# One order of an attention turn in place of two, with two places for other TensorE work that may stay empty

## The chip, the cores and the metric

The kernel runs on one core of a Trainium2 chip, in one launch. The metric is the time of the launch in microseconds as the device measures it; smaller is better. A core has a matrix engine (TensorE, "PE" in the profile, its weight loads "PEld"), a vector engine (VectorE, "DVE"), an engine for functions of one element (ScalarE, "ACT"), a general one (GpSimd, "POOL") and one that only issues transfers (SyncE, "SP"). Each runs its own instructions in the order in which they stand in its queue; semaphores hold an instruction back until another engine's result is there. TensorE writes its results into PSUM, which has eight banks of 128 x 512 fp32; a bank can be written anew once the engine that reads it is done.

## The reference

Two sequences of 1024 tokens, 512 wide, fp32. A block of the "macaron" kind: half a feed-forward step, attention, half a feed-forward step, each on the layer-normed input and added to the stream.

```python
x = x + 0.5 * ffn(layernorm(x))
x = x + attn(layernorm(x))
x = x + 0.5 * ffn(layernorm(x))

def ffn(x):      # W_base 512x512, 8 experts of rank 16, the best 2 of a softmax router
    probs = softmax(x @ W_router.T); topk_p, topk_i = top_k(probs, 2)
    w = one_hot(topk_i) weighted with topk_p / sum(topk_p)
    h = einsum('td,erd->ter', x, lora_A)
    return x @ W_base.T + b_base + 2.0 * einsum('ter,eor,te->to', h, lora_B, w)

def bitnet_linear(x, weight, scale):
    s = max(mean(abs(weight), axis=1), 1e-8)
    return nan_to_num((x @ sign(weight / s).T) * (s * scale), posinf=1e6, neginf=-1e6)

def attn(x):     # 32 heads of 16, 8 key/value heads, each shared by 4 query heads
    q, k, v = three bitnet_linear of x, split into heads
    p = softmax(q @ k.T / 4)
    return bitnet_linear(p @ v, o_weight, o_scale)
```

The attention matrix has 2 x 32 x 1024 x 1024 entries; everything else is small beside it.

## The kernel before

**Tiles.** A token tile is 128 tokens. Four of them are a group, so there are two sequences `b` with two groups `g` each. Attention is cut into 32 units: one unit is one sequence, one block of 512 queries and one key/value head with its 4 query heads.

**What a unit does.** Scores are made twice. First with the queries in the rows, to find the largest score of each query: 32 `m` tiles of 128 x 512 (`m_tile`, L785), each a single matmul on 64 rows of the array, each read by one VectorE reduce (`m_max`, L793). The maxima of a unit are gathered (`m_gather`), turned by a transpose on TensorE (`m_place`, tile `mp`, L805), copied by VectorE (`mT`) and moved by two DMAs on SP's queue into the rows of `mq` (L811). Then the scores are made again with the keys in the rows: 32 `e` tiles of 128 x 512 (`e_tile`), each of two matmuls into one bank: `e0`, keys against queries (L820), and `e1`, which takes the maxima off (L824). ScalarE reads each with an exponential into SBUF (`es`, L827). At last `A`: the exponentials times the values with a column of ones (`a_part`, L857), 16 matmuls of 32 columns for each pair of parts A0 A1 or A2 A3, into one bank of its own (`av`); when a unit is through, ScalarE copies that bank out (`unit_end`, L835), and only then may the next unit's first `A` write it. Heads with odd and even numbers lie on the upper and lower 64 rows of the array, so that two neighbouring `m` or `e` matmuls can run at the same time.

**Turns.** The loop of `attention` (L890) goes through turns. In turn n there are 8 `m` tiles of step n, 8 `e` tiles (16 matmuls) of step n-5 and four `A` parts of step n-6; four steps make a unit, so a unit's `m`, `e` and `A` overlap with those of its neighbours. Turns 0 to 4 have `m` tiles only (the lead-in), turns 128 to 133 have no `m` tiles any more. A unit's first `e` comes in a turn with n mod 4 = 1, its first `A` in one with n mod 4 = 2, `mp` in one with n mod 4 = 0.

**Banks.** Seven banks are shared by `m`, `e`, `mp` and all other TensorE work (`bank`, L53); the eighth is that of `av`. A new tile gets the bank that was given back longest ago in the program's order. Other work may hold up to two banks during attention (`flow.stock["fb"]`).

**Other work.** Layer norms, feed-forward steps, the projections and their cleaning of non-finite values run as strands, generators that yield the kind of engine they want next and a due time: `P` for TensorE, `v` VectorE, `a` ScalarE, `g` GpSimd, `d` a DMA on SP's queue. `Flow` keeps a counted time `flow.t` in ticks. When the loop calls `flow.offer(kind)`, the first strand that wants this kind, and is due, records its next instructions there. So the order of all queues is fixed when the program is built; nothing is chosen on the chip.

**The order of a turn.** A string gives it: `m0(i)`, `e0(i)`, `e1(i)` are single matmuls, `A0` to `A3` the four parts, `S` is `m_place`, and the letters F (TensorE), V and W (VectorE), C and D (ScalarE) are places where other work is offered; W and D are used only when more than one strand waits. There are two such strings. FULL has F at its front and its end. BARE has none, and begins with A0. At the start of a turn `wants` looks whether a TensorE piece will be due by the time of FULL's last place; if so the turn takes FULL and counts for 64 ticks (`TICK`), else BARE and 50 (`BRIEF`). `places` spreads the ticks over the order by `LOAD`.

**Waits written into the loop.** Before the first `A` of a unit, `until` offers all kinds, tick by tick, until the copy of the last unit's `av` has been recorded. Before a unit's queries and keys are fetched (`place`), `need` does the same until the projections that it reads have been recorded.

After the last turn the remaining strands are played out (`flow.play`), among them the output projection and second feed-forward step of the last group, which need the last unit.

Of the kernel before, what the change touches and what calls it, by code (L numbers as in the profile page):

```python
# [15 lines left out]
P = 128  # L16
D = 512
# [15 lines left out]
def macaron_kernel(ctx: ExitStack, tc: tile.TileContext, x_in, wbT, b_base, wrT, aT, bT,  # L33
                   wqT, q_sc, wkT, k_sc, wvT, v_sc, woT, o_sc, out):
    nc = tc.nc
    B, S, _ = x_in.shape
# [40 lines left out]
    for name, src, n_out in (("k", wkT, P), ("q", wqT, D), ("v", wvT, P), ("o", woT, D)):  # L77
# [5 lines left out]
        else:  # L83
            t = p2.tile([P, KC, GT], F32, tag="k", name=f"w_{name}", bufs=3)
# [36 lines left out]

    TICK, BRIEF = 64, 50
    LATER = {False: dict(Pv=10, Pa=10, PP=0, vP=36, aP=36, gP=40, va=20, av=16, vg=16, ag=14, gv=30,
                         ga=30, gg=0, vv=0, aa=0, dv=50, dg=50, da=50, dd=0, gd=32, vd=26, ad=26,
                         xd=50, dP=60),
# [12 lines left out]
    class Flow:  # L140
# [63 lines left out]
        def offer(self, kind):  # L204
# [12 lines left out]
                    self.settle()  # L217
                    return True
            return False

        def wants(self, kind, by):
            self.settle()
            return any(s.kind == kind and s.at <= by and (kind != "P" or self.lock in (None, s))
                       for s in self.strands)

        def crowd(self, kind):
            return sum(s.kind == kind and s.at <= self.t for s in self.strands)
# [11 lines left out]
    flow = Flow()  # L239
# [413 lines left out]
    def o_proj(b, g, hs, rank, mv, given, fast=False):  # L653
# [39 lines left out]
        for t in range(TG):  # L693
# [7 lines left out]

    FULL = ("V F W m0(3) e0(4) e0(7) e0(2) m0(7) e1(4) e1(7) e1(2) A0 A1 S C e0(6) e0(3) e1(6) "
            "e0(1) m0(4) V e1(1) m0(0) e1(3) A2 A3 m0(1) e0(0) C e0(5) m0(6) e1(5) e1(0) m0(5) D "
            "m0(2) F")
    BARE = ("A0 A1 e0(2) C m0(7) e1(2) e0(3) e0(4) e0(1) m0(0) e1(3) e1(1) C e1(4) m0(1) m0(6) S A2 "
            "A3 m0(3) e0(0) V e0(5) D e1(0) e0(7) e0(6) e1(5) m0(2) e1(7) V e1(6) W m0(5) m0(4)")
    LEAD_IN = ("m0(0) m0(6) m0(1) V m0(7) F C S V m0(4) m0(2) V F C m0(5) V F C V m0(3) V F C V")
    FULL, BARE, LEAD_IN = (  # L710
        [(o[0], int(o[1]) if len(o) > 1 else 0, int(o[3]) if len(o) > 2 else 0)
         for o in t.split()] for t in (FULL, BARE, LEAD_IN))
    LOAD = dict(e=1, m=1, A=4, F=10)

    def places(order, span):
        w = [LOAD.get(o[0], 0) for o in order]
        return [span * sum(w[:i]) // sum(w) for i in range(len(w))]

    at_F = places(FULL, TICK)[FULL.index(("F", 0, 0))]
    TU = NT // 2  # L720
    LEAD = TU + 1
    units = [(b, qb, g) for b in range(B) for qb in range(NQB) for g in range(G)]
# [40 lines left out]
    def place_v(u):  # L763

        b, _, g = units[u]
        v = p2.tile([P, NT, 32], F32, tag="vaug", name=f"vaug{u}", bufs=3)
        flow.pool = max(flow.pool, flow.t) + 5
        nc.gpsimd.memset(v[:, :, HD:32], 1.0)
        nc.gpsimd.tensor_copy(v[:, :, 0:HD], vd[b][:, :, g * HD:(g + 1) * HD])
        st[u]["v"] = v  # L770
# [9 lines left out]
    def m_tile(u, i, end=True):  # L780

        s = st[u]
        h, (qt, kh) = i % REP, m_where(u, i)
        s["m", i] = bank(f"m{u}_{i}")
        nc.tensor.matmul(s["m", i], s["q"][rows_of(h), h // 2, qt * P:(qt + 1) * P],  # L785
                         s["k"][rows_of(h), kh * 512:(kh + 1) * 512], start=True, stop=True)
        if end:
            m_max(u, i)
# [7 lines left out]
    def m_gather(u):  # L796
        mm = sm.tile([P, 4 * REP], F32, tag="mm", name=f"mm{u}", bufs=2)
        nc.vector.tensor_reduce(mm.rearrange("p (h t) -> p h t", h=REP), st[u]["mn"], AX.X, ALU.min)
        st[u]["mm"] = mm
# [14 lines left out]
    def e_tile(u, i, p):  # L814

        s = st[u]
        kt, h = i // REP, i % REP
        if p == 0:
            t = s["e", i] = bank(f"e{u}_{i}")
            nc.tensor.matmul(t, s["k"][rows_of(h), kt * P:(kt + 1) * P], s["q"][rows_of(h), h // 2, :],  # L820
                             start=True, stop=False)
        else:
            t = s["e", i]
            nc.tensor.matmul(t, two_r[rows_of(h), h // 2, :], s["mq"][rows_of(h), :], start=False,  # L824
                             stop=True)
            e = p2.tile([P, 512], F32, tag="es", name=f"es{u}_{i}", bufs=14)
            nc.scalar.activation(e, s.pop(("e", i)), AF.Exp, scale=HD ** -0.5)  # L827
            s["es"][i] = e
# [22 lines left out]
    def a_part(u, kt, half):  # L851
        s = st[u]
        if kt == 0 and half == 0:
            s["av"] = ps_a.tile([P, 512], F32, tag="av", name=f"av{u}")
        cols = slice(half * 256, half * 256 + 256)
        for h in range(REP):
            nc.tensor.matmul(s["av"][32 * h:32 * h + 32, cols], s["v"][:, kt, :],  # L857
                             s["es"][kt * REP + h][:, cols],
                             start=(kt + half == 0), stop=(kt + half == NT))
        if kt == NT - 1 and half == 1:  # L860
            flow.spawn(unit_end(u), -1)

    def todo(n, lead):

        k = n - lead
        return (k // TU, k % TU) if 0 <= k < TU * len(units) else None

    def attention(chains, n0):

        begin, span = flow.t, 0  # L870
        flow.free, flow.lock = False, None
        flow.busy = dict.fromkeys("Pvagd", flow.t)
        flow.stock["fb"] -= 4
        live = []

        def need(*keys):
            until(lambda: set(keys) <= ended)

        def until(cond):
            for _ in range(4000):  # L880
                flow.settle()
                if cond():
                    return
                flow.t += 1
                for kind in "Pvagd":
                    flow.busy[kind] = 0
                    flow.offer(kind)
            raise RuntimeError([(s.rank, s.kind, s.arg) for s in flow.strands])

        for n in range(n0, TU * len(units) + LEAD + 1):  # L890
            begin = flow.t = max(flow.t, begin + span)
            m, e, a = todo(n, 0), todo(n, LEAD), todo(n, LEAD + 1)
            live = [c for c in live if not c.done]
            while chains and len(live) < 3 and chains[0][0] <= n:
                live.append(flow.spawn(chains.pop(0)[1](), 9))
            if e and e[1] == 0:
                need(*[(units[e[0]][0], h, KC + 1) for h in range(NG)])
                place_v(e[0])
            order = (LEAD_IN if not e and not a else FULL if flow.wants("P", begin + at_F)
                     else BARE)  # L900
            span = BRIEF if order is BARE else TICK
            at = places(order, span)

            hold = n % TU == 0 and n // TU
            for pos, (kind, p, i) in enumerate(order):
                flow.t = max(flow.t, begin + at[pos])
                if kind == "m":
                    if m:
                        m_tile(m[0], m[1] * 2 * REP + i)
                elif kind == "e":  # L910
                    if e:
                        e_tile(e[0], e[1] * 2 * REP + i, p)
                elif kind == "A":
                    if a:
                        if a[0] and a[1] == p == 0:
                            until(lambda: "av" not in st[a[0] - 1])
                        a_part(a[0], a[1] * 2 + p // 2, p % 2)
                elif kind == "S":
                    if 0 < hold <= len(units):
                        m_place(hold - 1)  # L920
                    hold = 0
                elif kind == "F":
                    flow.offer("P")
                elif kind in "VW":
                    if kind == "V" or not m or flow.crowd("v") > 1:
                        flow.offer("v")
                elif kind in "CD":
                    if kind == "C" or not e or flow.crowd("a") > 1:
                        flow.offer("a")
                flow.offer("g")  # L930
                if not hold:
                    flow.offer("d")
            if m and m[1] == TU - 1:
                m_gather(m[0])
            if m and m[0] + 1 < len(units) and m[1] == 2:
                b, qb, g = units[m[0] + 1]
                need((b, qb, g // 2), *[(b, h, KC) for h in range(NG)])
                place(m[0] + 1)
        flow.free = flow.after = True
        flow.t = begin + span  # L940
        flow.stock["fb"] += 4
        flow.busy = dict.fromkeys("Pvagd", flow.t)
# [127 lines left out]
```

## Time and profile before

| | |
|---|---|
| median of 3 runs | 1160.85 us (1159.07 to 1164.19) |
| the profiled execution | 1162.21 us, of which 1160.2 us from the first to the last instruction (span) |
| mean granted TensorE clock | 0.968 |
| before turn 5 | 151.2 us |
| turns 5 to 127 | 151.2 to 1061.1 us |
| turns 128 to 133, without `m` | 1061.1 to 1092.5 us |
| after the last `av` matmul | 1092.5 to 1160.2 us |

A turn is taken from its first `m`, `e` or `av` matmul to that of the next turn. Which of the profile's matmuls belongs to which turn follows from the order of the program's TensorE instructions.

In the profile a line gives engine, source line, operation, the tile written and the tiles read, the shape and the count. In a timeline the first two columns are start and duration in us (several like instructions in a row are merged, their count at the end), and a bracket tells how long the engine stood idle before the instruction and what ended that wait. An fp32 matmul is shown as two instructions. The durations of matmuls overlap: 0.39 us is one matmul from its start to its end, while the next ones run in the array already, so distances between starts are the better measure.

### The profile page before, as it was taken

How to read it: one execution, taken by the hardware profiler on the slowest of the kernel's cores; microseconds unless marked ns; L12 is line 12 of the kernel's file. 1: busy time of each engine (PE TensorE's matmuls, PEld its weight loads, DVE VectorE, ACT ScalarE, POOL GpSimd, SP SyncE). 2: the span in 40 equal slices, each digit the busy share in tenths (PEclk: the TensorE clock that was granted, in tenths of full speed). 3: DMA queues.
4: the chain of work that ended last, by engine and by line, in shares of the span. 5: the costliest groups of instructions: out<-in, count | busy, mean ns of one | idle time of the engine just before them, and what ended most of it. 6: DMA issues, size and time to landing. Idle time of an engine off the chain costs nothing.

```text
span 1160.2 us, 21527 instructions
## 1 busy us (share of the span) xinstructions
PE 1068.2 (92%) x8453; PEld 589.0 (51%) x8453; DVE 878.5 (76%) x1694; ACT 669.8 (58%) x1309; POOL 287.6 (25%) x337
## 2 busy tenths in 40 slices
PE   3989679999999999999989899999999999999988
PEld 2446435554455554455555455644445555444544
DVE  5577978787788787778788898698779878874372
ACT  2222238765667566667746568665667766666611
POOL 4142632000110031112163322032011213421161
PEclk9989759999999999999989999999999999999989
DMA  8012453121111123214334342112222411221101
GB/s 272 3 61 77 140 174 105 47 47 47 47 47 47 47 83 118 48 40 106 106 87 144 83 114 57 47 47 56 56 65 64 120 45 36 67 84 47 55 24 50
DMA packets 48686, 87.43 MB, mean 75 GB/s; under 512 B 8760, under 2 KB 11832, under 8 KB 48584
## 3 DMA queue, kind: packets, MB, share of 16 engines
q1 hardware_dynamic: 47176, 83.36, 24.9%
q10 hardware_dynamic: 1152, 2.10, 0.5%
q8 instruction: 66, 1.08, 0.4%
q0 software_dynamic: 256, 0.59, 0.3%
q14 instruction: 36, 0.29, 0.1%
HBM read 51.19 MB, written 34.32 MB: 74 GB/s over the span
## 4 chain that ended last, share of the span: by engine, by line
PE 71%; DVE 18%; DMA 3%; ACT 3%; POOL 2%; issue 2%; SPq 0%; POOLq 0%; DVEq 0%; ACTq 0%
PE av L857 19%; PE m L785 15%; DVE mn L793 9%; PE e L820 9%; PE e L824 7%; PE pbf L444 5%; PE pbs L444 4%; PE po L668 2%; ACT es L827 2%; DMA x<-in_x 2%; PE pq L538 2%; PE pv L555 1%; PE pbf L448 1%; PE pbs L448 1%; PE phs L368 1%
## 5 line engine op out<-in xcount | busy, mean ns | idle before, releaser
L793 DVE TENSOR_REDUCE mn<-m 128x1 f32<-128x512 f32 x1024 | 647.6, 681 | 161.5 <-PE e L824 86.0
L827 ACT ACTIVATE es<-e 128x512 f32<-128x512 f32 x1024 | 542.4, 602 | 305.9 <-PE e L824 254.0
L785 PE MATMUL m<-k 64*128 64x512 f32 x1024 | 365.1, 443 | 27.6 <-DMA k<-kd 12.9
L857 PE MATMUL av<-es,vaug 128*32 128x256 f32 x4096 | 277.7, 389 | 18.9 <-ACT es L827 9.3
L820 PE MATMUL e<-k 64*128 64x512 f32 x1024 | 277.8, 443 | 2.7 <-DVE mn L793 2.5
L785 PEld LDWEIGHTS m<-k 64*128 64x128 f32 x1024 | 169.4, 188 | 175.9 <-DVE mn L793 77.8
L824 PE MATMUL e<-mq,two_r 64*128 64x512 f32 x1024 | 255.7, 399 | 1.9 <-DMA mq<-mT 1.9
L857 PEld LDWEIGHTS av<-es,vaug 128*32 128x32 f32 x4096 | 108.6, 110 | 148.8 <-issue 83.9
L820 PEld LDWEIGHTS e<-k 64*128 64x128 f32 x1024 | 121.8, 187 | 61.2 <-DVE mn L793 33.0
L824 PEld LDWEIGHTS e<-mq,two_r 64*128 64x128 f32 x1024 | 144.3, 187 | 14.4 <-issue 2.4
L444 PE MATMUL pbf<-wb,xTf 128*128 128x512 f32 x128 | 64.7, 636 | 0.0
L444 PE MATMUL pbs<-wb,xTs 128*128 128x512 f32 x128 | 61.4, 607 | 0.0
L459 POOL TENSOR_TENSOR x<-x,hbf 128x512 f32<-128x512 f32 x8 | 10.2, 1280 | 161.8 <-ACT hbf L456 161.8
L439 POOL TENSOR_TENSOR x<-x,bh 128x512 f32<-128x512 f32 x32 | 41.4, 1318 | 3.3 <-ACT xns L311 3.1
L444 PEld LDWEIGHTS pbf<-wb,xTf 128*128 128x128 f32 x128 | 24.4, 202 | 28.9 <-issue 27.8
L444 PEld LDWEIGHTS pbs<-wb,xTs 128*128 128x128 f32 x128 | 23.1, 192 | 27.4 <-issue 25.8
L270 POOL TENSOR_TENSOR ro<-ro,loo 128x512 f32<-128x512 f32 x16 | 20.7, 1294 | 58.2 <-DVE ro L268 51.5
L571 POOL TENSOR_TENSOR z<-z,y 128x512 fp32r<-128x512 f32 x17 | 22.7, 1337 | 49.9 <-ACT y L568 49.8
L568 ACT CAST y<-z 128x512 fp32r<-128x512 f32 x20 | 12.5, 626 | 36.5 <-DVE z L274 34.0
L265 POOL TENSOR_SCALAR loa<-y 128x512 f32<-128x512 f32 x17 | 11.7, 687 | 85.0 <-ACT y L543 84.2
L459 POOL TENSOR_TENSOR x<-x,hbs 128x512 f32<-128x512 f32 x8 | 10.3, 1285 | 88.5 <-ACT hbs L456 88.5
L620 POOL TENSOR_TENSOR an<-an,rb 128x512 f32<-128x512 f32 x15 | 19.7, 1316 | 49.8 <-DMA rb<-rd 49.7
(204 smaller groups left out, 1014.6 us busy)
## 6 DMA issues: line engine op xcount, KB each, us to landing
k<-qd SPq DMA_DIRECT2D x32, 512.0 KB
k<-kd SPq DMA_DIRECT2D x62, 256.0 KB
qd<-y SPq DMA_DIRECT2D x32, 256.0 KB
qd<-z SPq DMA_DIRECT2D x32, 256.0 KB
ad<-avs SPq DMA_DIRECT2D x32, 256.0 KB
x<-in_x SPq DMA_DIRECT2D x16, 256.0 KB
an<-ad SPq DMA_DIRECT2D x15, 256.0 KB
rb<-rd SPq DMA_DIRECT2D x15, 256.0 KB
```

The source lines that it names most:

```text
L439: nc.gpsimd.tensor_tensor(xt[:, t, :], xt[:, t, :], bh, ALU.add)
L444: nc.tensor.matmul(pb, xT[:, c, t * P:(t + 1) * P], wb[:, c, :], start=(c == 0), stop=False)
L448: nc.tensor.matmul(pb, hT[0][:, t * P:(t + 1) * P], lb, start=False, stop=True)
L538: nc.tensor.matmul(pq, w_[:, k, :], xs[j][:, k, :], start=(k + j == 0), stop=(k + j == KC))
L571: (nc.vector if fast else nc.gpsimd).tensor_tensor(lo, o, y, ALU.subtract)
L668: nc.tensor.matmul(po, hs[j][:, c, t * P:(t + 1) * P], wo[:, c, :], start=(c + j == 0), stop=(c + j == KC))
L785: nc.tensor.matmul(s["m", i], s["q"][rows_of(h), h // 2, qt * P:(qt + 1) * P], s["k"][rows_of(h), kh * 512:(kh + 1) * 512], start=True, st ...
L793: nc.vector.tensor_reduce(s["mn"][:, 2 * (h % 2) + h // 2, qt, kh:kh + 1], s.pop(("m", i)), AX.X, ALU.max, negate=True)
L820: nc.tensor.matmul(t, s["k"][rows_of(h), kt * P:(kt + 1) * P], s["q"][rows_of(h), h // 2, :], start=True, stop=False)
L824: nc.tensor.matmul(t, two_r[rows_of(h), h // 2, :], s["mq"][rows_of(h), :], start=False, stop=True)
L827: nc.scalar.activation(e, s.pop(("e", i)), AF.Exp, scale=HD ** -0.5)
L857: nc.tensor.matmul(s["av"][32 * h:32 * h + 32, cols], s["v"][:, kt, :], s["es"][kt * REP + h][:, cols], start=(kt + half == 0), stop=(kt + ...
```

## The change

FULL and BARE, `wants`, `places` and `TICK` go. One string, TURN, is used in every turn after the lead-in. It has F at its front and its end, and before its first A0 all `e` matmuls of six tiles and four `m` tiles. `offer` tells whether it gave something; the ticks of a turn are 48 and 8 more for each F that was used, so that a place with nothing to give adds none. The lead-in's string stays as it is, with the new count of ticks. The arithmetic, the tiles, the pools and the strands are the same.

```diff
-    TICK, BRIEF = 64, 50
+    BRIEF, SLICE = 48, 8
...
-        def wants(self, kind, by):
-            self.settle()
-            return any(s.kind == kind and s.at <= by and (kind != "P" or self.lock in (None, s))
-                       for s in self.strands)
...
-    FULL = ("V F W m0(3) e0(4) e0(7) e0(2) m0(7) e1(4) e1(7) e1(2) A0 A1 S C e0(6) e0(3) e1(6) "
-            "e0(1) m0(4) V e1(1) m0(0) e1(3) A2 A3 m0(1) e0(0) C e0(5) m0(6) e1(5) e1(0) m0(5) D "
-            "m0(2) F")
-    BARE = ("A0 A1 e0(2) C m0(7) e1(2) e0(3) e0(4) e0(1) m0(0) e1(3) e1(1) C e1(4) m0(1) m0(6) S A2 "
-            "A3 m0(3) e0(0) V e0(5) D e1(0) e0(7) e0(6) e1(5) m0(2) e1(7) V e1(6) W m0(5) m0(4)")
+    TURN = ("F e0(7) m0(6) e1(7) e0(2) e1(2) m0(1) D V e0(5) e0(4) e1(5) e1(4) e0(6) e0(3) e1(6) "
+            "e1(3) m0(5) m0(0) S A0 C V A1 m0(2) e0(1) e0(0) C m0(3) e1(0) e1(1) W m0(4) m0(7) A2 "
+            "A3 F")
...
-    LOAD = dict(e=1, m=1, A=4, F=10)
-
-    def places(order, span):
-        w = [LOAD.get(o[0], 0) for o in order]
-        return [span * sum(w[:i]) // sum(w) for i in range(len(w))]
-
-    at_F = places(FULL, TICK)[FULL.index(("F", 0, 0))]
+    LOAD = dict(e=1, m=1, A=4)
+    loads = {id(o): sum(LOAD.get(x[0], 0) for x in o) for o in (TURN, LEAD_IN)}
...
-            order = (LEAD_IN if not e and not a else FULL if flow.wants("P", begin + at_F)
-                     else BARE)
-            span = BRIEF if order is BARE else TICK
-            at = places(order, span)
+            order = LEAD_IN if not e and not a else TURN
+            done = given = 0
...
-            for pos, (kind, p, i) in enumerate(order):
-                flow.t = max(flow.t, begin + at[pos])
+            for kind, p, i in order:
+                flow.t = max(flow.t, begin + BRIEF * done // loads[id(order)] + SLICE * given)
+                done += LOAD.get(kind, 0)
...
-                    flow.offer("P")
+                    given += flow.offer("P")
...
+            span = BRIEF + SLICE * given
```

More of the change, by code (lines that the diff above doesn't have):

```diff
@@ L696, in o_proj @@
         flow.give(xT=1, xL=1)
-    FULL = ("V F W m0(3) e0(4) e0(7) e0(2) m0(7) e1(4) e1(7) e1(2) A0 A1 S C e0(6) e0(3) e1(6) "
-            "e0(1) m0(4) V e1(1) m0(0) e1(3) A2 A3 m0(1) e0(0) C e0(5) m0(6) e1(5) e1(0) m0(5) D "
-            "m0(2) F")
-    BARE = ("A0 A1 e0(2) C m0(7) e1(2) e0(3) e0(4) e0(1) m0(0) e1(3) e1(1) C e1(4) m0(1) m0(6) S A2 "
-            "A3 m0(3) e0(0) V e0(5) D e1(0) e0(7) e0(6) e1(5) m0(2) e1(7) V e1(6) W m0(5) m0(4)")
+    TURN = ("F e0(7) m0(6) e1(7) e0(2) e1(2) m0(1) D V e0(5) e0(4) e1(5) e1(4) e0(6) e0(3) e1(6) "
+            "e1(3) m0(5) m0(0) S A0 C V A1 m0(2) e0(1) e0(0) C m0(3) e1(0) e1(1) W m0(4) m0(7) A2 "
+            "A3 F")
     LEAD_IN = ("m0(0) m0(6) m0(1) V m0(7) F C S V m0(4) m0(2) V F C m0(5) V F C V m0(3) V F C V")
-    FULL, BARE, LEAD_IN = (
+    TURN, LEAD_IN = (
         [(o[0], int(o[1]) if len(o) > 1 else 0, int(o[3]) if len(o) > 2 else 0)
-         for o in t.split()] for t in (FULL, BARE, LEAD_IN))
-    LOAD = dict(e=1, m=1, A=4, F=10)
-    def places(order, span):
-        w = [LOAD.get(o[0], 0) for o in order]
-        return [span * sum(w[:i]) // sum(w) for i in range(len(w))]
-    at_F = places(FULL, TICK)[FULL.index(("F", 0, 0))]
+         for o in t.split()] for t in (TURN, LEAD_IN))
+    LOAD = dict(e=1, m=1, A=4)
+    loads = {id(o): sum(LOAD.get(x[0], 0) for x in o) for o in (TURN, LEAD_IN)}
     TU = NT // 2
```

## The prediction

> **What bounds the kernel now.** I read the page's busy rows and chain first, then the busy time by stage, then single turns on the timeline, then the waits.
>
> ```profile
> PE 1068.2 (92%) x8453; PEld 589.0 (51%) x8453; DVE 878.5 (76%) x1694; ACT 669.8 (58%) x1309; POOL 287.6 (25%) x337
> ...
> PE 71%; DVE 18%; DMA 3%; ACT 3%; POOL 2%; issue 2%; SPq 0%; POOLq 0%; DVEq 0%; ACTq 0%
> ```
> TensorE sets the end for 71% of the chain, VectorE for 18%; no other engine is near. By stage (columns: microseconds, then busy time of PE, weight loads, DVE, ACT, POOL, the granted clock, DMA share, GB/s):
>
> ```profile
> 151.20:181.80 30.60, 25.05 (x144) 12.56 (x142) 23.20 (x44) 15.95 (x30) 8.40 (x10) 0.63 0.58 200
> 181.80:571.00 389.20, 380.73 (x3327) 204.53 (x3326) 307.65 (x570) 262.59 (x507) 52.61 (x73) 1.00 0.23 62
> 571.00:602.70 31.70, 25.83 (x177) 16.49 (x177) 24.45 (x34) 13.57 (x26) 18.58 (x16) 0.89 0.39 125
> 602.70:1061.10 458.40, 440.76 (x3884) 239.16 (x3884) 371.25 (x683) 303.43 (x589) 113.76 (x129) 1.00 0.26 71
> ```
> The turns fill these stages. Turns 7 to 127 take 886 us: 84 in the full order, 37 in the bare one. The second and fourth rows are nearly all TensorE; the third holds two turns (62, 63) that last 31.7 us. One clean full turn on PE (it ends where the next begins, at 464.51):
>
> ```profile
> 457.20 0.49 PE L785 MATMUL m<-k 64*128 64x512 f32 x1
> 457.77 0.39 PE L785 MATMUL m<-k 64*128 64x512 f32 x1
> 458.32 1.07 PE L857 MATMUL av<-es,vaug 128*32 128x256 f32 x16
> 459.32 0.50 PE L820 MATMUL e<-k 64*128 64x512 f32 x2
> 460.45 1.07 PE L857 MATMUL av<-es,vaug 128*32 128x256 f32 x16
> 461.45 0.49 PE L785 MATMUL m<-k 64*128 64x512 f32 x1
> 462.25 0.42 PE L785 MATMUL m<-k 64*128 64x512 f32 x2
> 462.59 1.12 PE L448 MATMUL pbf<-lb,hTf 128*128 128x512 f32 x2
> ```
> It lasts 7.31 us: 5.39 of its own and 1.92 of other work at the end (two fp32 matmuls, two passes each). Matmuls on the two halves of the rows run in pairs: a pair every 0.23 us, 0.33 for the first after another kind of work and 0.32 to the next kind, 1.00 for 16 `av` matmuls. The other engines' pace in the same turn: VectorE starts a reduce 0.53 us after its `m` (0.46 if that isn't first in its block) and one per 0.60, each 0.68 long; ScalarE starts an exponential 0.46 us after the second `e` matmul and one per 0.49, each 0.60 long.
>
> What a missing bank does is seen in a bare turn, VectorE above TensorE:
>
> ```profile
> 677.35 1.97 DVE L793 TENSOR_REDUCE mn<-m 128x1 f32<-128x512 f32 x3 [0.58 <-PE m L785]
> 678.08 0.52 PE L785 MATMUL m<-k 64*128 64x512 f32 x2
> 678.53 1.07 PE L857 MATMUL av<-es,vaug 128*32 128x256 f32 x16
> ```
> The eighth tile of that block takes the bank that the first reduce frees: 677.35+0.69+0.06 = 678.10, and it starts at 678.10; the `av` block follows 0.45 after it instead of 0.32. So a bank is written 0.055 us after its reader ends, and I can lay out a turn by hand. For the full order, which opens 5, 5 and 6 tiles between its `av` blocks, this gives no wait with six banks, as measured.
>
> **The change, part by part.** No instruction is added or removed. Counted in the two programs' orders, 66 turns of the new one (61 before) carry about 2 us of other work at their boundary, 20 about 1 us, 30 none.
>
> *1. Turns with 2 us of other work.* The new turn opens ten tiles (e7 m6 e2 m1 e5 e4 e6 e3 m5 m0) in 1.71 us before its first `av` block. While other work holds a bank, six are left. From the paces above, 0 being the turn's first pair: reduces of m6, m1 start at 0.53, 1.13; exponentials at 0.80 (e7), 1.29, 1.78, 2.27, 2.76, 3.25 (e3). The seventh tile gets m6's bank at 1.27 (due 1.25), the eighth e7's at 1.45 (due 1.25), the last two e2's and m1's at 1.95 (due 1.71). A0 starts at 2.39, not 2.04. In the second block m3 takes e3's bank, 3.25+0.60+0.06 = 3.91 (due 3.72); the last `av` block ends at 5.80. With 1.92 of other work 7.72, against 7.31: +0.41. Ends: without any wait the layout gives 5.14+1.92 = 7.06 (-0.25); with one more late release +0.5. I take +0.40 x 66 = +26 (-16 to +33). What hid this before was the `av` block between small groups of tiles; that cover is now behind the ten.
>
> The row for a switch between kinds of matmul is 0.32 to 0.34 against 0.23, so 0.1 each. The Trainium skill (TensorEngine Tiling (Array Packing), Key Properties) says that changing the tiling mode drains TensorE; the new order has five changes a turn for six, so by this rule alone the term would be 66 x -0.1 = -7. The same page (PSUM Bottleneck) says that packing speeds up TensorE but not the emptying of PSUM; that rule speaks against the change, and the bare turn's row is a case of it: by it the +26 stands. The trace measures both; the wait is the larger.
>
> *2. The copy of `av` (L835) ahead of a unit's first `av` matmul.* It is queued on ScalarE, and A0 waits for it. Before, two units pay at a bare turn's start, and others inside full turns:
>
> ```profile
> 875.47 0.62 ACT L835 COPY avs<-av 128x512 f32<-128x512 f32 x1
> 876.18 1.07 PE L857 MATMUL av<-es,vaug 128*32 128x256 f32 x16 [1.65 <-POOL ro L270]
> ```
> (The page names POOL, which had long finished; the copy ends at 876.09.) The seven such places cost about 11 us (turns 70, 118, 38 stand 2.6, 2.0, 1.5 over a clean full turn with as much other work). In the new order the copy of nine units stands behind six exponentials of its turn: 0.80+6x0.49+0.62 = 4.4, where A0 was due at 2.4: 2.0 each, less 0.96 in four of them, where an other matmul falls into the gap: +14. The other 22 have it behind two: A0 barely moves, but e3's release comes 0.49 later and with it m3: 0.4 each, +9. Net +12 (0 to +20). Behind A0 on PE stands everything.
>
> *3. Two banks held.* Ten turns begin after two transposed tiles, and one in five of the base-matmul turns after one tile's end and the next one's start: five banks, so e4 too waits for 1.27 (due 0.79). Some 18 turns x 0.5, less what such turns already lose (the 18 full turns with 0.3 to 1.8 us of other work stand 0.8 over): +5 (0 to +10).
>
> *4. Maxima to `mq`.* `mp` moves right before A0. The one row that waits for it shows 4.5 us from its start to the first matmul on the landed rows (149.87 to 154.38, 1.95 of it idle). In the seven units with no other work behind it the next such matmul is due after 3.8: +0.7 each, +5 (0 to +7). The two DMAs stay on SP's queue in the same company.
>
> *5. Turns without other work.* By hand 5.55 against the bare turn's 5.41: 30 x 0.14 = +4 (0 to +8).
>
> *6. Seams.* A bare turn after a full one waits for the exponentials of the full turn's last tiles:
>
> ```profile
> 655.02 1.07 PE L857 MATMUL av<-es,vaug 128*32 128x256 f32 x16 [1.00 <-ACT es L827]
> ```
> 14 such seams stand 0.2 to 2.0 over, about 1 in the middle. With one order A0 is 2 us into the turn: -13 (-9 to -16).
>
> *7. The forced stretch, 571 to 602.7.* Other work overdue for the next unit was played out at once: 31.7 against 2 x 5.41 + 11.8 of other work = 22.6. The new order gives this work out over turns 58 to 63: -9 (-5 to -10).
>
> *8. Lead-in.* At 156.8 the statistics of a token tile still on its way from DRAM stand in VectorE's queue (3.87 us idle), and `m` tiles behind them. They now come a turn later: -5 (-7 to 0).
>
> *9. End.* 28 matmuls move ahead of the last `av` block, 2 us into turns 124 to 127, 4 us into 128 and 129, which last 6.5 us for 4.3 of their own and hide them. After it, base matmuls of 5.1 us fall into the wait at 1125.48 instead of behind it:
>
> ```profile
> 1125.48 1.97 PE L319 MATMUL pts<-ident,xns 128*128 128x128 f32 x8 [5.57 <-ACT xns L311]
> ```
> -5 + 2 = -3 (-5 to +2).
>
> Sum: 26+12+5+5+4-13-9-5-3 = +22. The profiled execution took 1162.2 us, 1160.2 of it span; 1182 of span and the 2.0 around it are 1184, and the median of the runs shown is 1.4 below the profiled one: **1183 us**, 1.9% slower.
>
> **Rivals.** *A, faster:* the ten tiles find their banks in time, because ScalarE and VectorE rest during the 2 us of other work. For it: both have a slack, 4.8 us of reduces and 3.9 of exponentials in a turn of 7.3. Against it: the bare turn's wait, with seven banks and eight tiles. Terms 1, 3 and 5 then are -16, 0, 0, and all together -29; with half of the -16, -21. It decides from a turn of 7.45 down: all terms but 1 and 3 make -9, so these two may cost 0.14 a turn. I put it at 1160.8-21 = 1140. *B, slower still:* the copy of `av` is late in all 31 units, since other evictions stand ahead of it on ScalarE: 31 x 1.5 = 46 in place of 23: 1206. *C, nothing:* both orders have their two places at the same turn boundary, and what the seams give the banks take: 1161.
>
> **How the numbers follow.** Forecast 0.51, A 0.22, B 0.13, C 0.14. Half-widths of the terms (24, 10, 5, 4, 4, 4, 3, 4, 3), put together as independent, are 28, so 1155 to 1211 for the likeliest alone; below, it is stretched to A: **1140 to 1208**. By 0.5% (5.8 us, what a measurement of this kernel can tell from none): faster 0.22, same 0.14, slower 0.64. A's best and a full B are left out.
>
> **What would show it.** Right: boundary-loaded turns of 7.6 to 7.8 us; `m` and `e` on PE waiting for `es` and `mn`; A0 idle behind the copy in turns 30, 74, 102, 122; no turn over 12 us at 571 to 602; the last `av` to the end in 63 us instead of 67.7. Wrong: such turns at 7.1 to 7.4, which gives A, or ScalarE idle less and TensorE no more, which gives C.

## The result, and the profile after

| | before | changed |
|---|---|---|
| median of 5 runs | 1160.85 us (1159.07 to 1164.19) | 1172.65 us (1170.5 to 1176.68) |
| ratio, 95% interval | | 1.010 (1.0077 to 1.0124) |
| profiled execution, span | 1162.21, 1160.2 us | 1174.61, 1172.8 us |
| start of turn 7 | 175.0 us | 168.5 us |
| turns 7 to 127 | 886.1 us | 908.9 us |
| turn 128 to the end | 99.1 us | 95.4 us |

The change makes the kernel slower, by 11.8 us of medians (12.6 between the two profiled spans), half of the 22 forecast; 1172.65 lies inside the range. The page of the changed kernel, its busy rows and the chain by engine:

```profile
PE 1094.3 (93%) x8453; PEld 606.5 (52%) x8453; DVE 864.0 (74%) x1694; ACT 661.2 (56%) x1309; POOL 286.8 (24%) x337
...
PE 74%; DVE 15%; DMA 4%; issue 2%; POOL 2%; ACT 2%; SPq 1%; POOLq 0%; DVEq 0%; ACTq 0%
```

TensorE has the same 8453 instructions and is "busy" for 26 us more: short waits for a bank are counted in its busy time (turn 43, below, is 7.69 us long and shown as busy throughout, with matmuls that took 7.31 before), so this loss is hardly seen in the list of waits. By stage (microseconds; then busy time of PE, weight loads, DVE, ACT, POOL; the granted clock; DMA share; GB/s), turns 9 to 57, 58 to 63, and 64 to 127:

```profile
183.50:557.08 373.58, 361.49 (x3030) 196.39 (x3029) 276.45 (x520) 236.34 (x462) 51.90 (x66) 0.99 0.23 64
557.08:606.49 49.41, 49.38 (x413) 29.65 (x410) 36.76 (x66) 29.39 (x58) 12.59 (x15) 1.00 0.31 87
606.49:1077.43 470.94, 460.68 (x3897) 248.00 (x3897) 368.05 (x689) 304.28 (x597) 121.90 (x138) 0.99 0.26 70
```

The middle row is the old forced stretch: turns 58 to 63 take 49.4 us with 14.6 us of other work; before, they took 60.7 with the same 14.6. The gain is there, and the two long stages lose more.

A turn with 2 us of other work, turn 43, on PE (it ends at 453.99):

```profile
446.30 0.50 PE L809 MATMUL e<-k 64*128 64x512 f32 x1
446.30 0.50 PE L774 MATMUL m<-k 64*128 64x512 f32 x1
...
447.11 0.40 PE L809 MATMUL e<-k 64*128 64x512 f32 x2
447.34 0.40 PE L813 MATMUL e<-mq,two_r 64*128 64x512 f32 x2
447.61 0.60 PE L809 MATMUL e<-k 64*128 64x512 f32 x2
447.95 0.49 PE L813 MATMUL e<-mq,two_r 64*128 64x512 f32 x2
448.21 0.50 PE L774 MATMUL m<-k 64*128 64x512 f32 x2
448.64 1.07 PE L846 MATMUL av<-es,vaug 128*32 128x256 f32 x16
449.64 0.50 PE L774 MATMUL m<-k 64*128 64x512 f32 x1
...
451.07 1.07 PE L846 MATMUL av<-es,vaug 128*32 128x256 f32 x16
452.07 1.98 PE L439 MATMUL pbf<-wb,xTf 128*128 128x512 f32 x4
```

It lasts 7.69 us. The first six tiles come at the pair's pace; the seventh (447.61, due 447.57) and those behind it come later and later, and A0 starts at 448.64, which is 2.34 into the turn, where the hand layout has 2.39 (2.04 without waits). The second `av` block ends at 452.07, 5.77 in, against 5.80 by hand. The readers of the banks in the same turn:

```profile
446.87 1.29 DVE L782 TENSOR_REDUCE mn<-m 128x1 f32<-128x512 f32 x2 [1.98 <-PE m L774]
447.07 3.05 ACT L816 ACTIVATE es<-e 128x512 f32<-128x512 f32 x6 [2.68 <-PE e L813]
```

The first reduce takes 0.69, ends at 447.56 and frees a bank; the seventh tile starts 0.05 later. The first exponential takes 0.60 and ends at 447.67; the eighth tile (the second of the row at 447.61) starts at 447.72.

A turn in which the copy of `av` (now L824) stands behind six exponentials, turn 74, without other work:

```profile
675.71 3.25 ACT L816 ACTIVATE es<-e 128x512 f32<-128x512 f32 x6 [0.75 <-PE e L813]
...
677.55 0.50 PE L774 MATMUL m<-k 64*128 64x512 f32 x2
...
678.82 0.62 ACT L824 COPY avs<-av 128x512 f32<-128x512 f32 x1
...
679.54 1.91 PE L846 MATMUL av<-es,vaug 128*32 128x256 f32 x16 [1.49 <-issue]
```

TensorE stands still for 1.49 us until the copy has ended (678.82 + 0.62 = 679.44). The label says "issue": the profile shows no releaser, and it is the row on ScalarE that tells what was awaited. The `av` block then takes 1.91 instead of 1.07. The stretches around it, same columns as above:

```profile
677.00:679.50 2.50, 1.04 (x7) 0.43 (x6) 2.46 (x6) 2.44 (x5) 0.00 (x0) 1.00 0.08 25
679.50:681.40 1.90, 1.86 (x18) 0.77 (x18) 0.66 (x2) 0.00 (x0) 1.09 (x2) 0.53 0.49 148
681.40:682.80 1.40, 1.40 (x9) 1.14 (x8) 0.60 (x1) 0.00 (x0) 0.39 (x2) 0.50 0.97 230
```

After the pause the granted clock is half for 3.4 us. The turn lasts 9.30 us.

### The profile page after: what moved, and what is told of

It is laid out like the page before. It is cut to its first block, busy times and chain, and to the rows that moved or that the text cites. A ratio compares the mean times of both kernels' runs of the same rounds, so it can differ in the third digit from the quotient of the medians.

```text
span 1172.8 us, 21556 instructions
## 1 busy us (share of the span) xinstructions
PE 1094.3 (93%) x8453; PEld 606.5 (52%) x8453; DVE 864.0 (74%) x1694; ACT 661.2 (56%) x1309; POOL 286.8 (24%) x337
## 4 chain that ended last, share of the span: by engine, by line
PE 74%; DVE 15%; DMA 4%; issue 2%; POOL 2%; ACT 2%; SPq 1%; POOLq 0%; DVEq 0%; ACTq 0%
PE av L846 19%; PE e L809 13%; PE m L774 13%; PE e L813 8%; DVE mn L782 8%; PE pbf L439 5%; PE pbs L439 4%; PE po L663 2%; PE pq L533 2%; DMA k<-kd 2%; PE phs L363 1%; PE pbf L443 1%; PE pv L550 1%; DMA x<-in_x 1%; ACT es L816 1%
## 5 line engine op out<-in xcount | busy, mean ns | idle before, releaser
L774 PE MATMUL m<-k 64*128 64x512 f32 x1024 | 350.9, 450 | 14.5 <-DMA k<-kd 13.3
L809 PE MATMUL e<-k 64*128 64x512 f32 x1024 | 335.3, 451 | 3.5 <-DVE mn L782 0.4
L846 PE MATMUL av<-es,vaug 128*32 128x256 f32 x4096 | 277.8, 389 | 12.6 <-issue 11.2
L813 PE MATMUL e<-mq,two_r 64*128 64x512 f32 x1024 | 276.3, 404 | 7.4 <-DMA mq<-mT 5.4
L774 PEld LDWEIGHTS m<-k 64*128 64x128 f32 x1024 | 156.3, 189 | 127.7 <-ACT es L816 70.1
L809 PEld LDWEIGHTS e<-k 64*128 64x128 f32 x1024 | 149.8, 186 | 120.0 <-DVE mn L782 54.8
L813 PEld LDWEIGHTS e<-mq,two_r 64*128 64x128 f32 x1024 | 141.3, 187 | 16.4 <-DMA mq<-mT 6.0
L615 POOL TENSOR_TENSOR an<-an,rb 128x512 f32<-128x512 f32 x15 | 19.2, 1284 | 110.0 <-DMA rb<-rd 110.0
L619 POOL TENSOR_TENSOR anxL<-an,anxT 128x512 fp32r<-128x512 f32 x15 | 19.1, 1283 | 67.0 <-ACT anxT L617 67.0
L265 POOL TENSOR_TENSOR z<-z,loa 128x512 f32<-128x512 f32 x17 | 21.7, 1276 | 48.6 <-DVE z L263 23.1
L663 PE MATMUL po<-sign_o,anxT 128*128 128x512 f32 x64 | 28.1, 439 | 1.9 <-ACT anxT L637 1.9
```

The lines of the kernel that those rows point to most:

```text
L265: nc.gpsimd.tensor_tensor(o, o, lo_, ALU.add)
L663: nc.tensor.matmul(po, hs[j][:, c, t * P:(t + 1) * P], wo[:, c, :], start=(c + j == 0), stop=(c + j == KC))
```

## The experiments

To compare kernels I cut each profiled execution at turn 7 and turn 128, and call *excess* what a turn lasts beyond the time that TensorE's matmuls for other work cover in it and beyond 5.33 us (5.24 where n mod 4 = 0), about the least of the kernel before. *Steady* turns are 16 to 127 without 58 to 65. All in us, worked out from the traces:

| | to turn 7 | excess 7-15 | excess steady | excess 58-65 | other work 7-127 | from turn 128 | span | median |
|---|---|---|---|---|---|---|---|---|
| before | 175.0 | 3.4 | 48.6 | 14.8 | 177.1 | 99.1 | 1160.2 | 1160.85 |
| changed | 168.5 | 10.7 | 74.1 | 4.2 | 177.8 | 95.4 | 1172.8 | 1172.65 |
| copy in front | 168.2 | 9.7 | 60.3 | 4.0 | 177.2 | 95.1 | 1156.8 | 1160.39 |
| spread | 167.0 | 9.3 | 41.1 | 3.3 | 175.4 | 104.0 | 1142.4 | 1146.8 |
| before, copy in front | 173.2 | 3.5 | 40.4 | 29.2 | 176.5 | 114.0 | 1179.1 | 1180.6 |
| spread, 50 and 7 | 168.1 | 8.9 | 41.1 | 12.0 | 175.1 | 97.6 | 1145.1 | 1146.8 |
| before, spread bare order | 172.6 | 3.7 | 41.7 | 7.3 | 175.2 | 103.3 | 1146.1 | 1147.73 |
| spread, 50 and 9 | 178.7 | 4.2 | 44.5 | 3.4 | 174.5 | 99.8 | 1147.4 | 1145.27 |
| changed, half reads | 164.7 | 6.7 | 1.4 | -1.2 | 177.8 | 92.2 | 1083.9 | 1085.65 |
| spread, half reads | 162.1 | 6.3 | 9.2 | 1.0 | 175.3 | 101.9 | 1098.2 | 1100.02 |

(A row's parts and 121 turns of 5.33 or 5.24 add up to its span. The half-read kernels have one time each. A row but for its median is one execution, and the times of one kernel lie 2 to 8 us apart, so a difference of 1 us between two rows shows nothing by itself.)

**Copy in front.** In the changed kernel the copy of a unit's `av` is recorded before anything else of the turn in which the next unit's first A stands; with "a" the loop of `until` offers ScalarE alone, the copy first and at once:

```diff
             hold = n % TU == 0 and n // TU
+            if a and a[0] and a[1] == 0:
+                until(lambda: "av" not in st[a[0] - 1], "a")
             for kind, p, i in order:
```

> The changed kernel with the copy of a unit's av bank recorded at the very front of the turn of the next unit's first A, ahead of that turn's exponentials. In the changed kernel the 30 turns with n mod 4 = 2 stand 39.5 us over a clean full turn plus their other work, all other turns 0.54 us each; so the copy theory (the copy behind 2 or 6 exponentials holds A0 or, through e3's bank, m3) gives these 30 turns 39.5 - 30 x 0.54 = 23 us back: 1172.6 - 23 = 1150 us, such turns with 2 us of other work at 7.7 instead of 8.35, and turns 30, 74, 102, 122 at about 5.6 instead of 9.0. Rival, bank theory alone (these turns are long because of the ten tiles, and the copy only ends last): under 8 us back, 1165 or more, and the turns stay at 8 or over.

Measured: 1160.39 us, ratio to the kernel before 0.999 (0.9978 to 1.0002). Turn 74 in this kernel:

```profile
672.29 0.58 ACT L824 COPY avs<-av 128x512 f32<-128x512 f32 x1 [0.17 <-issue]
672.88 3.04 ACT L816 ACTIVATE es<-e 128x512 f32<-128x512 f32 x6
...
674.87 1.07 PE L846 MATMUL av<-es,vaug 128*32 128x256 f32 x16
```

The copy is over before the first exponential could start, the `av` block takes 1.07 again, and the turn lasts 5.90 us instead of 9.30. Over the 30 turns with n mod 4 = 2 the excess falls from 39.5 to 16.3, by the 23 expected, and turns 30, 74, 102 and 122 last 6.03, 5.90, 5.75 and 5.96. But the total fell by 12: the other turns rose from 49.4 to 57.7, by 2.7 in turn 56 alone, where keys were waited for (2.2 us). So the copy theory holds for the place, and about a third came back elsewhere, because the other work is given out in another order.

**Spread.** The old full order as the only one, places passed over when empty:

```diff
-    TURN = ("F e0(7) m0(6) e1(7) e0(2) e1(2) m0(1) D V e0(5) e0(4) e1(5) e1(4) e0(6) e0(3) e1(6) "
...
+    TURN = ("V F W m0(3) e0(4) e0(7) e0(2) m0(7) e1(4) e1(7) e1(2) A0 A1 S C e0(6) e0(3) e1(6) "
+            "e0(1) m0(4) V e1(1) m0(0) e1(3) A2 A3 m0(1) e0(0) C e0(5) m0(6) e1(5) e1(0) m0(5) D "
+            "m0(2) F")
```

> The changed kernel with the string of the old full order as its only order: places for other TensorE work at the front and the end, passed over when empty, the new ticks; 5, 5 and 6 tiles between the av blocks instead of ten and six. In this order the copy of av too comes ahead of the next unit's exponentials, so it is to be read against the kernel with the copy in front (1150 expected). Burst theory: 69 turns with 2 us of other work lose their 0.38, so 26 us less, and the turns without other work keep no seam: about 1122 us, loaded turns at 7.3. Rival, the ten tiles cost nothing of their own and the copy was all: 1150 and loaded turns at 7.6 or more. Second rival: VectorE, with nothing to wait for, becomes the bound in turns without other work (8 reduces of 0.68 and one more operation are 6.1 us): 1135.

Measured: 1146.8 us, 0.9881 (0.9854 to 0.9908); faster than both kernels. Turns with 1.98 us of base matmuls last 7.28 to 7.31 in 18 of 29 cases; with the copy in front and the order of ten tiles none was under 7.66. The steady excess falls by 19.2. The burst theory's turns are right and its total is 25 us too low. The second rival explains a part of that: in 11 of the 26 steady turns without other work VectorE is busy for over 95% of the turn, ScalarE in none. Turn 75 here, VectorE (it lasts from 662.73 to 668.97):

```profile
662.58 2.48 DVE L782 TENSOR_REDUCE mn<-m 128x1 f32<-128x512 f32 x4
664.97 0.69 DVE L274 BATCH_NORM_STATS2 sto<-x 128x6 f32<-128x512 f32 x1
665.69 0.18 DVE L275 BATCH_NORM_AGGREGATE mvs<-sto 128x2 f32<-128x6 f32 x1
665.79 1.85 DVE L782 TENSOR_REDUCE mn<-m 128x1 f32<-128x512 f32 x3
667.56 0.16 DVE L288 TENSOR_SCALAR ves<-mvs 128x4 f32<-128x4 f32 x1
667.62 0.69 DVE L782 TENSOR_REDUCE mn<-m 128x1 f32<-128x512 f32 x1
```

One row ends where the next begins: 6.04 of the turn's 6.23 us are VectorE's.

**Before, copy in front.** The same edit in the kernel before.

> The kernel before with the same copy in front. Seven places there paid about 11 us for a late copy: copy theory 1150 us. Its forced stretch at turn 62 is still there, with 14.7 us of other work in place of 10.7. Rival, another wait takes the copy's place in those turns: 1157 to 1161.

Measured: 1180.6 us, 1.0155 (1.0138 to 1.0172). Both expectations missed the total. In the steady turns the excess falls by 8.2, near the 11 of the theory. But the forced stretch has 14.2 us of other work in turn 62 (10.5 before) and its turns stand 14 us further over, and the strands after the last turn take 15 us more. The waits of TensorE in this last part:

```profile
PE hwps L428 <- DVE tops L390: 10.3, 1, 10.3
PE pts L319 <- ACT xns L311: 9.6, 4, 7.1
PE av L857 <- POOL x L686: 2.2, 1, 2.2
```

(Total, number, longest, us.) In the kernel before, the two upper ones were 0 and 5.6: there no matmul had to wait so long for the router's top values of the last tokens. That moving 31 copies on one engine reorders the last strands is seen; by which step of the planner it does was not followed.

**Spread, 50 and 7 ticks.** `BRIEF, SLICE = 50, 7` in the spread kernel.

> The kernel with the spread order, but 50 ticks a turn and 7 for each place that was used, which are the old ticks (50 and 64). By the program's order this alone brings the forced stretch back: 11.7 us of other work at once in turn 62 (3.0 with 48 and 8). Stretch theory: in the old kernel turns 58 to 63 lasted 60.7 us, in the changed one 49.4 with as much other work (14.6 each), so 11 us more than the spread kernel. Rival, the stretch's price was that of the old orders around it and not of playing the work out at once: within 3 us of the spread kernel.

Measured: 1146.8 us, 0.986 (0.9841 to 0.9879), the median of the spread kernel. Turns 62 and 63, here and (second fence) in the spread kernel:

```profile
568.50:600.71 32.21, 26.43 (x185) 17.40 (x184) 26.61 (x36) 13.83 (x25) 18.79 (x16) 0.89 0.26 72
```

```profile
570.72:587.57 16.85, 16.65 (x134) 9.74 (x133) 14.65 (x24) 11.05 (x21) 7.78 (x7) 1.00 0.41 125
```

The stretch is back, with TensorE idle for 5.0 us and the clock at 0.50 from 590.9 to 597.7, and costs 8.7 us of excess (12.0 against 3.3) beyond the work that is in it. The total doesn't show it, since the last part is 6.4 us shorter, by another order of the same strands. The stretch theory is right about the turns, the rival about the time.

**Before, spread bare order.** The kernel before; BARE becomes FULL without its F's.

> The kernel before, its bare order replaced by the full one without its places for other TensorE work; the choice between the two strings and their 64 and 50 ticks stay. So no seam is left between two orders of tiles, and the copy of av stands ahead of the next unit's exponentials, while work is still given out by the old rule. Seam theory (the prediction's: 13 us for seams and 11 for late copies): 1160.9 - 13 - 11 = 1137 us. Rival, VectorE bounds the turns with little other work: in the kernel before, the turns with under 1.7 us of it stand 54.8 us over, 8.4 of them in turn 63 (the forced stretch, which stays); in the one-order kernel with spread tiles, which has neither seam nor late copy, such turns still stand 41.6 over; so 54.8 - 8.4 - 41.6 = 5 less: 1156 us.

Measured: 1147.73 us, 0.9884 (0.9861 to 0.9907), between the two. Of the 16 us that its turns gain, 7.5 are excess of turns 58 to 65 (turn 62 has 5.7 us of other work here) and 6.9 steady excess, where the rival had 5 and the seam theory 24. So the two-order kernel could be had as quick as the one-order kernel: the tile order counts, not the number of orders.

**Half reads.** In the changed kernel and in the spread one, every reader of an `m` or `e` bank takes half the tile. These kernels leave out half of the scores, so they give times only, not the reference's result:

```diff
-        nc.vector.tensor_reduce(s["mn"][:, 2 * (h % 2) + h // 2, qt, kh:kh + 1], s.pop(("m", i)), AX.X, ALU.max,
+        nc.vector.tensor_reduce(s["mn"][:, 2 * (h % 2) + h // 2, qt, kh:kh + 1], s.pop(("m", i))[:, 0:256], AX.X, ALU.max,
...
-            nc.scalar.activation(e, s.pop(("e", i)), AF.Exp, scale=HD ** -0.5)
+            nc.scalar.activation(e[:, 0:256], s.pop(("e", i))[:, 0:256], AF.Exp, scale=0.01 * HD ** -0.5)
...
-                             s["es"][kt * REP + h][:, cols],
+                             s["es"][kt * REP + h][:, 0:256],
```

> The changed kernel in which VectorE takes the maximum over half of each m tile and ScalarE the exponential of half of each e tile (the scores scaled by 0.01, so that it stays finite with wrong maxima), and A multiplies that half twice. TensorE has the same matmuls in the same order; only the banks come free sooner. Bank theory: the ten tiles no longer wait, and turns with 1.98 us of base matmuls fall from 7.67 to 7.06 (the hand layout without waits) to 7.2. Rival, the 0.38 is TensorE's own, from the order of its kinds of matmul: they stay at 7.6 or more.

> The spread order with the same halved reads (maxima and exponentials of half a tile, scores scaled by 0.01, A on that half twice). Bank theory: it had no waits to lose in turns with 2 us of other work, which stay at 7.3, so that here the order of the changed kernel is the quicker one by its one change of kind less. Turns without other work, 0.7 over a clean one in the spread kernel, fall to within 0.2 of it if VectorE bounds them, and stay if a seam does.

Measured: 1085.65 and 1100.02 us. The reduce falls from 681 to 418 ns, the exponential from 613 to 391. Turn 42 of the changed order:

```profile
412.18 0.50 PE L809 MATMUL e<-k 64*128 64x512 f32 x1
...
413.45 0.43 PE L809 MATMUL e<-k 64*128 64x512 f32 x2
413.69 0.43 PE L813 MATMUL e<-mq,two_r 64*128 64x512 f32 x2
413.91 0.43 PE L774 MATMUL m<-k 64*128 64x512 f32 x2
414.28 1.07 PE L846 MATMUL av<-es,vaug 128*32 128x256 f32 x16
...
419.32 0.50 PE L809 MATMUL e<-k 64*128 64x512 f32 x1
```

The ten tiles follow each other at the pair's pace, A0 starts 2.10 in (2.34 above), the turn lasts 7.14. In the spread order the same kind of turn stays at 7.28 to 7.31. With the readers' times cut, TensorE's matmuls unchanged, the burst's cost is gone and the changed order is the quicker by 0.15 a turn: the loss was the banks. The spread order's turns without other work in the steady part, their own work alone, fall from 5.99 to 5.50 us in the mean, to within 0.2 of a clean one, so the readers' pace had held them. Both readers were cut at once, so this doesn't part VectorE from ScalarE; that VectorE is the one rests on the busy shares above.

**Spread, 50 and 9 ticks.** `BRIEF, SLICE = 50, 9`.

> The spread order with 50 ticks a turn and 9 for each used place: by the program's order no turn has more than 3.7 us of other work, and no two such stand close. Stretch theory: with 50 and 7 turn 63 alone stood 8.3 over; here it stands under 1.5 over, and the time is that of the spread kernel, 1140 to 1147. Rival, the time of the turns stays and the strands after the last turn decide: more than 4 us from it, either way.

Measured: 1145.27 us, 0.9858 (0.9838 to 0.9879). Turn 63 has no excess, and the time is that of the spread kernel within the intervals. With 1146.8, 1146.8 and 1147.7 of the three others that spread the tiles, 1145 to 1148 is what this order gives under four rules of giving out work.

## Why the prediction was right, and where its sizes were off

The steady excess splits along four kernels between the two: before 48.6, copy in front 40.4 (-8.2), one spread order with the new ticks 41.1 (+0.7; 41.7 with the old ones), the ten tiles with the copy in front 60.3 (+19.2), the copy back behind the exponentials 74.1 (+13.8).

1. *The burst* (+26; with the terms 3 to 5, which fall in the same step, +40): right in its mechanism. The loaded turn lasts 7.65 to 7.71 us in its clean cases against 7.72 by hand, and the half reads show that it was the banks. The sign named for it, waits of `m` and `e` for `es` and `mn`, makes only 0.6 us of the list of waits, since such waits stand in the busy time. As a sum it was twice too large: +19.2. The turns with 2 us of other work pay it (their excess over turns 7 to 127, copy in front: 34.6 with the ten tiles, 11.8 spread), which is near the +26 of term 1. The turns with less do not: they stand 38.3 over with the ten tiles and 41.6 spread (14.1 spread with half reads). The terms 3 and 5 had been priced against clean turns, and these turns were not clean in either order: the pace of the banks' readers held them.
2. *The copy* (net +12): +13.8 - 8.2 = +6. Place and number were right: the 30 turns that hold the copy carry 23 us of it, the gross sum foretold. The price of a place was not: turns 30, 74, 102 and 122 stand 3.6 to 4.0 over, not 2.0, since the halved clock comes on top of the pause. Turns 22, 26, 46 and 90, where a matmul of other work runs in the gap, keep a granted clock of 1.00 and stand 1.0 over. Turn 54, the ninth with the copy behind six exponentials, paused 1.20 us at a clock of 1.00 and stands 1.5 over. But with the copy in front some 9 of the 23 came back in other turns; the sum had no such give-back.
4. *Maxima to `mq`* (+5): six waits of 2.0 us together from 190 us on, the longest 0.8; the waits are there, at less than half the sum.

```profile
PE av L846 <- issue: 10.4, 8, 2.0
PE e L813 <- DMA mq<-mT: 2.0, 6, 0.8
```

(Changed kernel, 190 to 1077 us. The first line is the late copies.)

6. *Seams* (-13): the step that failed. The row that showed a seam was right: the waits of `av` for `es`, 8.3 us in 13 places in the kernel before, are gone. In the kernel before with its copies in front they are still there (total, number, longest; first the kernel before, 190 to 1061 us, then with the copy in front, 190 to 1065):

```profile
PE av L857 <- ACT es L827: 8.3, 13, 1.1
```

```profile
PE av L857 <- ACT es L827: 7.5, 11, 1.1
```

But from this kernel to the spread one, which has none, the steady excess moved by +0.7, not -13. The prediction took the end of a wait for a gain in time. The next limit stood close behind: with half reads the spread order's steady excess falls from 41.1 to 9.2, so it was the pace of the banks' readers. Of the two VectorE is the likelier, by its busy share; no run parts them.
7. *The forced stretch* (-9): -10.6. Longest turn in 557 to 606: 9.58 us.
8. *Lead-in* (-5): -6.5 to turn 7, and all given back by turn 15 (+7.3 of excess). In turn 9 TensorE waits 3.4 us for `mq`: its rows were issued at 180.59 and landed at 187.40, and after the wait the clock falls (0.75 over the rest of the turn). Before, they were issued 4.2 us later, at 184.76, and the first matmul on them ran 4.9 us after that without a wait. So the transfer was issued earlier but took 6.8 us; why wasn't followed, and the prediction named no next wait here.
9. *End* (-3): -3.7. From the last `av` to the end 65.8 us, where 63 was foretold; the rest of the gain (1.8) lies in turns 128 to 133, where the term had a loss, so its parts were wrong and its sum came right by luck.

Together: +25.5 (steady) + 7.3 - 10.6 + 0.7 of more other work - 6.5 - 3.7 = +12.7, where +22 was foretold. The steady part was forecast at +39: the burst with its companions 20.8 too much, the copy 6.4 too much, the seams 13.7 too little. So the forecast of "slower" rested on the right two causes; that its sum came as near as it did was partly luck, since two errors of size stood against the seams, which gave nothing.

Rival A (ten tiles find their banks) fell by its own test, 7.45: loaded turns last 7.67. It comes true only with half reads. Rival B's copy is late in all units only by a little: 25 of the 30 turns that hold it stand at most 1.1 over. Rival C, no change, falls with the interval, 1.0077 to 1.0124.

## What to carry to other kernels

An order of tiles is priced by laying out its banks against the readers' pace; a burst longer than the free banks pays at each turn that nothing else holds, and the same order wins once the readers are quicker. Ending a wait is worth no more than the distance to the next limit of the same turn, so write that limit beside each gain. Where a planner places other work, compare kernels by stage: a moved copy shifted the last strands by 15 us, more than the edit under study, and a total alone would have blamed the copy.

## What the hardware showed

In the four turns with a late copy and nothing to run in the gap, a pause of TensorE of 1.46 to 1.98 us halved the granted clock for 3.4 us (turn 74: 1.49 us of pause, then 0.53 and 0.50; turn 102: 1.98, then 0.56). The Trainium skill (TensorE: Matmul & The Clock Gate, What's actually happening) puts the fall after at least one idle window of about 3.4 us; the measurement decides, and shorter pauses did it here. The length alone doesn't settle it: in the kernel before, the pause of 1.65 us ahead of 876.18 left the clock at 1.00, and so did four pauses of 1.36 to 1.70 us in that kernel with the copy in front; a pause of 1.70 us in turn 87 of the spread kernel halved it. In the turns where a few matmuls of other work ran in the gap it stayed at 1.00 too. In the ten traces every change of the clock lies on one grid of 3.41 us, and each stretch at half clock is a whole number of such steps (679.6 to 683.0 in turn 74), so where a pause falls against the grid, and what else TensorE does in that step, may count. What decides was not tried.

Half the elements cost a reduce 61% of its time (418 of 681 ns) and an exponential 64% (391 of 613).
